# Input transposes of a TensorE-bound graph kernel: 128x128 on TensorE, or 32x32 blocks on VectorE behind a second, blocked load

## Chip, cores, metric

One core of one Trainium2 chip. The metric is the device time of one execution in microseconds, as the median of several; all runs told of here were in the fast state (granted TensorE clock 0.994 to 0.997 of full speed).

## The reference

Two graph layers on 64 graphs of 256 nodes with 256 features, all in float32. Layer 0 is a graph attention twice over (scores masked by `adj`, softmax over axis 1), a layer norm and a feed-forward part; layer 1 is attention with 8 heads, whose values depend on the relation `adj == r`, and a feed-forward part again. Cut to what uses the inputs:

```python
def _gat(h, adj, W, a, out_features):
    Wh = jnp.matmul(h, W)
    e = leaky_relu(Wh @ a[:F] + swapaxes(Wh @ a[F:], 1, 2), 0.2)
    att = softmax(where(adj > 0, e, NEG), axis=1)
    return jnp.matmul(att, Wh)
# layer 1
for r in range(4):
    mask = (adj_matrix == r)[:, None]
    out = out + einsum('bhij,bhjd->bhid', attn * mask, v_r)
```

## The kernel before

It takes two graphs at a time (a group, 512 nodes) and runs 32 turns. A turn works on three groups: on layer 1 of group y, layer 0 of group x, and the input and first attention of group z. The projection needs x with features on partitions (`xT`); both layers need the adjacency with the other node on partitions (`aT`). TensorE made both, sixteen 128x128 transposes for a group, into PSUM (where the results of TensorE land), and ScalarE or VectorE copied the result to SBUF (the memory in which the kernel keeps its tiles):

```python
def to_features(src, name, scale=None, shift=None):
    dst = work.tile([P, KB, TN], F32, tag="hT", name=name)
    for k in range(KB):
        ps = bank(f"{name}p{k}")
        for t in range(T):
            nc.tensor.transpose(ps[:, t * P:(t + 1) * P], src[:, t, k * P:(k + 1) * P], ident)
        ...  # VectorE: copy (or scale and shift) ps to dst
def adjacency(u, af):
    for b in range(G):
        ps = bank(f"aTp{u}_{b}")
        ...  # four TensorE transposes of af into ps
        nc.scalar.copy(aT[:, b * NB:(b + 1) * NB, :]..., ps)
    # check that every entry is 0 or 1 (the narrow path relies on it)
    nc.vector.scalar_tensor_tensor(a, a, 1.0, a, op0=ALU.subtract, op1=ALU.mult, accum_out=other[:, u:u + 1])
def early(z):
    d["aT"] = adjacency(z, d["af"])
    d["xT"] = to_features(d["xs"], f"xT{z}")
# the turn, from the middle on (order of TensorE):
#   hid 6,7 (h1p) -> early(z) -> apply 2, 3 (po, zo) -> out 0 (yop) -> project(z) (xpp) -> out 1 (yop) -> ...
```

`apply` ends in `divided` on VectorE: the reciprocal `rz` of `zo`, then `oT = po * rz`, which the second `yop` matmuls read.

Of the kernel before, what the change touches and what calls it, by code (L numbers as in the profile page):

```python
# [9 lines left out]
F32 = mybir.dt.float32  # L10
I32 = mybir.dt.int32
# [5 lines left out]
P = 128  # L17
# [368 lines left out]
def narrow_path(  # L386
# [13 lines left out]
    nc = tc.nc  # L400
    B, N, F = x.shape
# [3 lines left out]
    KB = F // P  # L405
    FB = FF // P
    NB = N // P
    G = 2
    T = G * NB
    TN = G * N  # L410
# [7 lines left out]
    io = ctx.enter_context(tc.tile_pool(name="io", bufs=2))  # L418
    work = ctx.enter_context(tc.tile_pool(name="work", bufs=2))
# [3 lines left out]
    def bank(name):  # L423
        return psum.tile([P, 512], F32, tag="g", name=name, bufs=6)


    def load(u):
        xs = io.tile([P, T, F], F32, tag="xs", name=f"xs{u}")
        nc.sync.dma_start(xs, x[G * u:G * (u + 1)].rearrange("b (c p) f -> p (b c) f", p=P))
        if u == 1:  # L430

            af = work.tile([P, FB, TN], F32, tag="h1", name=f"af{u}", bufs=1)
            af = af[:, 0:2, :].rearrange("p c (t n) -> p (c t) n", t=2)
        else:
            af = io.tile([P, T, N], F32, tag="af", name=f"af{u}", bufs=1)
        nc.gpsimd.dma_start(af, adj[G * u:G * (u + 1)].rearrange("b (c p) f -> p (b c) f", p=P))
        return xs, af


    ident = const.tile([P, P], F32, name="ident")  # L440
# [75 lines left out]

    gwe = gat_weights()
    g = {u: {} for u in range(NG)}
    for u in range(2):
        g[u]["xs"], g[u]["af"] = load(u)  # L520
    wf1, wf2 = weight(g_wf1, "wf1"), weight(g_wf2, "wf2")
    lg1, lb1, bf1, lg2, lb2, bq, bk, lg3, lb3, b1 = columns(
        (g_g1, g_b1, g_bf1, g_g2, g_b2, t_bq, t_bk, t_g1, t_be1, t_b1), "cols", nc.scalar)
# [20 lines left out]
# [7 lines that stand above are left out]
            if scale is None:  # L551
                nc.vector.tensor_copy(dst[:, k, :], ps)
            else:
                nc.vector.tensor_scalar(dst[:, k, :], ps, scale[:, k:k + 1], shift[:, k:k + 1],  # L554
                                        op0=ALU.mult, op1=ALU.add)
        return dst

    def adjacency(u, af):

        aT = work.tile([P, T, N], F32, tag="aT", name=f"aT{u}")  # L560
        for b in range(G):
            ps = bank(f"aTp{u}_{b}")
            for j in range(NB):
                for i in range(NB):
                    nc.tensor.transpose(ps[:, j * N + i * P:j * N + (i + 1) * P],  # L565
                                        af[:, b * NB + i, j * P:(j + 1) * P], ident)
            nc.scalar.copy(aT[:, b * NB:(b + 1) * NB, :].rearrange("p t n -> p (t n)"), ps)
        a = af.rearrange("p t n -> p (t n)")
        nc.vector.scalar_tensor_tensor(a, a, 1.0, a, op0=ALU.subtract, op1=ALU.mult,
                                       accum_out=other[:, u:u + 1])  # L570
        return aT

    def projected(u, hT):
        xp = work.tile([P, T, WX], F32, tag="wh", name=f"xp{u}")
# [179 lines left out]
    def early(z):  # L754

        d = g[z]
        d["aT"] = adjacency(z, d["af"])
        d["xT"] = to_features(d["xs"], f"xT{z}")

    def project(z):  # L760
        d = g[z]
# [6 lines left out]
    def second_scores(z):  # L768
        d = g[z]
        d["s"] = gat_softmax(z, 1, d["hp"], F, F, d["aT"])  # L770
# [38 lines left out]
    def turn(y_, x_, z):  # L809
        def have(u):  # L810
            return 0 <= u < NG

        if y_ == 0:
            g[z]["xs"], g[z]["af"] = load(z)
        if z + 1 < NG:
            g[z + 1]["xs"], g[z + 1]["af"] = load(z + 1)
        Y, X, Z = g.get(y_, {}), g.get(x_, {}), g.get(z, {})
        if have(y_):
            hT = to_features(Y["y"], f"h2T{y_}", lg2, lb2)
        if have(x_) and y_ > 0:  # L820
            second_sums(x_)
        if have(y_):
            q, k_ = queries_keys(y_, hT)
            v = values(y_, hT, range(T // 2))
        if have(x_):
            h1hT = to_features(X["y"], f"h1T{x_}", lg1, lb1)
        if have(y_):
            values(y_, hT, range(T // 2, T), v)
            quads = [(b, m) for b in range(G) for m in range(KB)]
            aT = Y["aT"]  # L830
            oT = work.tile([P, KB, TN], F32, tag="oT", name=f"oT{y_}", bufs=1)
            acc = [None] * G
            e = {}

            def scores(n):
                e[n] = weighted(y_, *quads[n], q, k_, aT)

            def apply_(n):
                b, m = quads[n]
                if m == 0:  # L840
                    acc[b] = [psum.tile([P, 512], F32, tag=t_, name=f"{t_}{y_}_{b}") for t_ in ("po", "zo")]
                applied(b, m, v, *e.pop(n), *acc[b])
                if m == KB - 1:
                    divided(y_, b, *acc[b], oT)

        h1 = None

        def steps():
            if have(y_):
                yield scores, 0  # L850
            yield hid, range(0, 3)
            if have(y_):
                yield scores, 1
                yield piece, None
                yield apply_, 0
            yield hid, range(3, 4)
            if have(y_):
                yield scores, 2
                yield apply_, 1
            yield hid, range(4, 6)  # L860
            if have(y_):
                yield scores, 3
                yield piece, None
            yield hid, range(6, 8)
            if have(z):
                yield early, z
            if have(y_):
                yield apply_, 2
                yield apply_, 3

        def hid(blocks):
            nonlocal h1
            if have(x_):
                h1 = hidden(x_, 0, h1hT, wf1, bf1, AF.Relu, blocks, h1)

        for do, what in steps():
            do(what)
        if have(y_):
            yo = work.tile([P, T, F], F32, tag="y", name=f"yo{y_}")

            def out_(b):
                add_blocks(y_, "yop", yo, Y["res"], b, lambda t, k: oT[:, k, t * P:(t + 1) * P],
                           lambda b, k: wo[:, k, :], KB)
            out_(0)
            piece()
        if have(z):
            project(z)
        if have(y_):
            out_(1)
        if have(z):  # L890
            first_scores(z)
        if have(y_):
            yn = normed(y_, 2, yo)
            res = affine(y_, 2, yn, rg3, rb3)
            piece()
        if have(x_):
            yf = hidden_out(x_, 0, h1, wf2, X["res"])
            X["y"] = normed(x_, 1, yf)
            X["res"] = affine(x_, 1, X["y"], rg2, rb2)
        if have(y_):  # L900
            hT = to_features(yn, f"h3T{y_}", lg3, lb3)
        if have(z):
            Z["hp"] = gat_first(z, Z["s"], Z["xp"])
        if have(y_):
            h1 = hidden(y_, 1, hT, w1, b1, AF.Gelu, range(FB))
        if have(z):
            second_scores(z)
        if y_ == NG - 2:
            left.append(out_pieces(y_, h1, res))
        elif y_ == NG - 1:  # L910
            for _ in out_pieces(y_, h1, res):
                pass
        else:
            yf = hidden_out(y_, 1, h1, w2, res)
            yn = normed(y_, 3, yf)
            res = affine(y_, 3, yn, rg4, rb4)
            nc.sync.dma_start(out[G * y_:G * (y_ + 1)].rearrange("b (c p) f -> p (b c) f", p=P), res)
# [2 lines left out]
        g[z]["hp"] = gat_first(z, g[z]["s"], g[z]["xp"])  # L920

    with tc.manual_schedule(engines={mybir.EngineType.PE}):
        for stage in (early, project, first_scores):
            stage(0)
        for stage in (early, project, first_scores):
            stage(1)
        for stage in (first_sums, second_scores):
            stage(0)
        for stage in (first_sums, second_scores):
            stage(1)  # L930
        second_sums(0)
        hT = to_features(g[0]["y"], "h1T0", lg1, lb1)
        h1 = hidden(0, 0, hT, wf1, bf1, AF.Relu, range(FB))
        yf = hidden_out(0, 0, h1, wf2, g[0]["res"])
        g[0]["y"] = normed(0, 1, yf)
        g[0]["res"] = affine(0, 1, g[0]["y"], rg2, rb2)
        second_sums(1)
        for u in range(NG):
            turn(u, u + 1, u + 2)
# [11 lines left out]
    ps = bank("goodp")  # L951
# [42 lines left out]
```

## Time and profile before

| | before |
|---|---|
| time, median of 6 (range) | 3344.96 us (3344.36 to 3345.93) |
| TensorE busy (share of the span) | 3298.2 us (99%) |
| VectorE / ScalarE / GpSimd busy | 54% / 32% / 30% |
| DMA queue q1, share of 16 engines | 3.8% |

A busy share tells which engine leaves least room; the chain that ended last tells whether the end of the program hangs on that engine. The prediction shows the lines. Mean durations of matmuls overlap, so what one costs in a stream is read from the starts of its neighbours, not from its duration. In a timeline, a bracket at the end of a line gives how long the engine was idle before it, and what ended that.

### The profile page before, as it was taken

How to read it: one execution, taken by the hardware profiler on the slowest of the kernel's cores; microseconds unless marked ns; L12 is line 12 of the kernel's file. 1: busy time of each engine (PE TensorE's matmuls, PEld its weight loads, DVE VectorE, ACT ScalarE, POOL GpSimd, SP SyncE). 2: the span in 40 equal slices, each digit the busy share in tenths (PEclk: the TensorE clock that was granted, in tenths of full speed). 3: DMA queues.
4: the chain of work that ended last, by engine and by line, in shares of the span. 5: the costliest groups of instructions: out<-in, count | busy, mean ns of one | idle time of the engine just before them, and what ended most of it. 6: DMA issues, size and time to landing. Idle time of an engine off the chain costs nothing.

```text
span 3342.7 us, 43294 instructions
## 1 busy us (share of the span) xinstructions
PE 3298.2 (99%) x17948; PEld 2160.2 (65%) x17948; DVE 1818.6 (54%) x3611; ACT 1083.8 (32%) x1920; POOL 987.4 (30%) x852
## 2 busy tenths in 40 slices
PE   7999999999999999999999999999999999999998
PEld 5666666666666666666666666666666666666655
DVE  3654556555556545565555565455654555654545
ACT  3233233332332333333323333333333233333321
POOL 2223323233232233232332322332323323223222
PEclk9999999999999999999999999999999999999999
DMA  4000000000000000000000000000000000000000
GB/s 131 14 19 14 20 7 20 20 13 20 7 20 20 20 13 20 7 20 20 13 20 7 20 20 20 13 18 8 20 20 13 20 7 20 20 14 12 1 7 14
DMA packets 57258, 60.92 MB, mean 18 GB/s; under 512 B 1976, under 2 KB 56416, under 8 KB 57056
## 3 DMA queue, kind: packets, MB, share of 16 engines
q1 hardware_dynamic: 39808, 41.03, 3.8%
q0 software_dynamic: 16896, 16.78, 2.3%
q8 instruction: 143, 2.34, 0.3%
q14 instruction: 59, 0.48, 0.0%
q10 hardware_dynamic: 352, 0.28, 0.0%
HBM read 41.31 MB, written 16.78 MB: 17 GB/s over the span
## 4 chain that ended last, share of the span: by engine, by line
PE 97%; DVE 1%; issue 1%; DMA 1%; POOL 0%; SPq 0%; ACT 0%; ACTq 0%; POOLq 0%; DVEq 0%
PE h1p L668 27%; PE yfp L627 25%; PE po L737 7%; PE vp L700 7%; PE sp L716 4%; PE yop L627 3%; PE qp L687 3%; PE hpp L616 3%; PE xpp L578 3%; PE kp L687 3%; PE ygp L627 3%; PE zo L740 2%; PE rows L588 1%; PE aTp L565 1%; PE yfp L794 1%
## 5 line engine op out<-in xcount | busy, mean ns | idle before, releaser
L670 ACT ACTIVATE h<-h1p,cols 128x512 f32<-128x512 f32 x512 | 353.2, 690 | 531.7 <-PE h1p L668 530.5
L668 PE MATMUL h1p<-h1T,wf 128*128 128x512 f32 x1024 | 474.5, 607 | 0.1
L627 PE MATMUL yfp<-wf,h 128*128 128x256 f32 x2048 | 447.3, 379 | 0.0
L668 PE MATMUL h1p<-h3T,w 128*128 128x512 f32 x1024 | 445.4, 592 | 1.8 <-DVE h3T L554 1.8
L724 DVE TENSOR_TENSOR ea<-e,aT 128x1024 f32<-128x1024 f32 x256 | 320.2, 1291 | 197.6 <-ACT e L722 197.6
L627 PEld LDWEIGHTS yfp<-wf,h 128*128 128x128 f32 x2048 | 386.8, 190 | 51.8 <-issue 0.5
L627 PE MATMUL yfp<-w,h 128*128 128x256 f32 x1920 | 419.4, 379 | 0.0
L627 PEld LDWEIGHTS yfp<-w,h 128*128 128x128 f32 x1920 | 362.5, 190 | 48.1
L722 ACT ACTIVATE e<-sp 128x512 f32<-128x512 f32 x512 | 264.3, 603 | 301.3 <-PE sp L716 300.0
L668 PEld LDWEIGHTS h1p<-h3T,w 128*128 128x128 f32 x1024 | 194.2, 190 | 234.2 <-issue 228.6
L746 POOL TENSOR_TENSOR low<-low,rz 128x512 f32<-128x512 f32 x64 | 82.2, 1284 | 891.0 <-DVE rz L745 891.0
L668 PEld LDWEIGHTS h1p<-h1T,wf 128*128 128x128 f32 x1024 | 184.9, 190 | 232.7 <-issue 190.6
L597 DVE SCALAR_TENSOR_TENSOR s<-s 128x512 f32<-128x512 f32 x128 | 87.1, 680 | 427.9 <-ACT s L594 426.6
L658 POOL TENSOR_TENSOR res<-res,rb 128x1024 f32<-128x1024 f32 (+1 forms) x130 | 301.3, 2317 | 10.2
L630 DVE TENSOR_TENSOR yf<-yfp,res 128x512 f32<-128x512 f32 x124 | 85.8, 692 | 394.8 <-PE yfp L627 393.6
L645 POOL TENSOR_TENSOR rs<-ve,mhalf 128x4 f32<-128x4 f32 (+1 forms) x130 | 131.6, 1012 | 411.9 <-DVE ve L644 411.8
L745 DVE RECIPROCAL rz<-zo 128x512 f32<-128x512 f32 x64 | 214.7, 3354 | 59.7 <-PE zo L740 59.6
L700 PE MATMUL vp<-wv,h2T 128*128 128x512 f32 x512 | 230.1, 592 | 0.0
L689 ACT ACTIVATE q<-qp,cols 128x512 f32<-128x512 f32 x64 | 44.0, 687 | 530.4 <-PE qp L687 530.4
L618 ACT COPY hp<-hpp 128x258 f32<-128x258 f32 x128 | 47.4, 376 | 423.6 <-PE hpp L616 423.6
L657 POOL TENSOR_TENSOR res<-yf,rg 128x1024 f32<-128x1024 f32 (+1 forms) x66 | 151.2, 2291 | 96.2 <-DVE yf L649 95.4
L700 PEld LDWEIGHTS vp<-wv,h2T 128*128 128x128 f32 x512 | 94.9, 190 | 107.6 <-issue 107.6
(494 smaller groups left out, 4351.1 us busy)
## 6 DMA issues: line engine op xcount, KB each, us to landing
xs<-in_x_dram SPq DMA_DIRECT2D x32, 512.0 KB, 3.9
af<-in_adj_dram POOLq DMA_DIRECT2D x32, 512.0 KB, 4.5
out_dram<-res SPq DMA_DIRECT2D x30, 512.0 KB
wf<-in_L_gnn_w_ff_dram SPq DMA_DIRECT2D x2, 1024.0 KB, 7.1
w<-in_L_gnn_W_dram SPq DMA_DIRECT2D x2, 1024.0 KB
out_dram<-res SPq DMA_DIRECT2D x4, 256.0 KB, 2.1
wv<-in_L_gnn_Wv_dram SPq DMA_DIRECT2D x2, 256.0 KB
gw<-in_L_gnn_W_dram ACTq DMA_DIRECT2D x1, 256.0 KB
```

Of the source, the lines that this page charges most:

```text
L627: nc.tensor.matmul(ps[:, i * F:(i + 1) * F], lhs(t, k), rhs(b, k), start=(k == 0), stop=(k == n - 1))
L657: nc.gpsimd.tensor_mul(r, xn, g[:, None, :].to_broadcast(list(r.shape)))
L658: nc.gpsimd.tensor_add(r, r, b[:, None, :].to_broadcast(list(r.shape)))
L668: nc.tensor.matmul(ps, wi[:, k, f * P:(f + 1) * P], hT[:, k, :], start=(k == 0), stop=(k == KB - 1))
L670: nc.scalar.activation(h1[:, f, :], ps, func, bias=bi[:, f:f + 1])
L687: nc.tensor.matmul(ps, w[:, k, m * P:(m + 1) * P], hT[:, k, :], start=(k == 0), stop=(k == KB - 1))
L700: nc.tensor.matmul(ps, hT[:, k, t * P:(t + 1) * P], wvf[:, k, :], start=(k == 0), stop=(k == KB - 1))
L716: nc.tensor.matmul(ps[a][:, j * N:(j + 1) * N], k_[hp, m, j0:j0 + P], q[hp, m, b * N:(b + 1) * N], start=True, stop=True)
L722: nc.scalar.activation(e[:, a, :], ps[a], AF.Exp, scale=isd)
L724: nc.vector.tensor_tensor(ea[:, a:a + 2, :], e[:, a:a + 2, :], ab[:, None, :].to_broadcast([P, 2, NB * N]), ALU.mult)
L737: nc.tensor.matmul(po[hp, m * N:(m + 1) * N], vs[:, hp], w[:, a, j * N:(j + 1) * N], start=(n == 0), stop=(n == len(terms) - 1))
L745: nc.vector.reciprocal(rz, zo)
```

## The change

Its intent is to take the input transposes of the middle turns off TensorE. The VectorE transpose that the kernel uses turns 32x32 blocks and leaves each within its 32 partitions. So the load does the moving between groups of partitions: for each quarter q of the partitions it brings pieces of 32 columns, so that the blocks that quarter needs lie beside one another; VectorE then transposes all blocks of a tile in one instruction. x is loaded a second time for this, since the residual needs it untransposed. The first two groups keep the old way.

```diff
 def load(u):
     xs = io.tile([P, T, F], F32, tag="xs", name=f"xs{u}")
     nc.sync.dma_start(xs, x[G * u:G * (u + 1)].rearrange("b (c p) f -> p (b c) f", p=P))
-    af = io.tile([P, T, N], F32, tag="af", name=f"af{u}", bufs=1)      # u == 1: in the h1 tile
-    nc.gpsimd.dma_start(af, adj[G * u:G * (u + 1)].rearrange("b (c p) f -> p (b c) f", p=P))
+    xq = io.tile([P, KB, TN], F32, tag="xq", name=f"xq{u}", bufs=1)
+    aq = io.tile([P, T, N], I32, tag="aq", name=f"aq{u}", bufs=1)
+    xu = x[G * u:G * (u + 1)].rearrange("b (n r) (k q c) -> q k r (b n) c", r=32, k=KB, c=32)
+    au = adj[G * u:G * (u + 1)].rearrange("b (n r) (j q c) -> q b r j n c", r=32, j=NB, c=32)
+    for q in range(Q):
+        qp = slice(q * 32, (q + 1) * 32)
+        for k in range(KB):
+            nc.sync.dma_start(xq[qp, k, :].rearrange("r (n c) -> r n c", c=32), xu[q, k])
+        for b in range(G):
+            nc.sync.dma_start(aq[qp, b * NB:(b + 1) * NB, :].rearrange("r j (n c) -> r j n c", c=32), au[q, b])
 def adjacency(u, aq):
+    aT = work.tile([P, T, N], I32, tag="aT", name=f"aT{u}")
+    nc.vector.transpose(aT..., aq...)
+    return aT
 def early(z):
-    d["aT"] = adjacency(z, d["af"])
-    d["xT"] = to_features(d["xs"], f"xT{z}")
+    d["xT"] = work.tile([P, KB, TN], F32, tag="hT", name=f"xT{z}")
+    nc.vector.transpose(d["xT"]..., d["xq"]...)
+    d["aT"] = adjacency(z, d["aq"])
# cut: load_first, early_first (groups 0 and 1 as before, both adjacency tiles in the h1 tile);
#      checked(), the check of the adjacency, now a function of its own;
-            oT = work.tile([P, KB, TN], F32, tag="oT", name=f"oT{y_}", bufs=1)
+            oT = q                                   # room for the new tiles
```

More of the change, by code (lines that the diff above doesn't have):

```diff
@@ L424, in bank @@
         return psum.tile([P, 512], F32, tag="g", name=name, bufs=6)
+    Q = P // 32
     def load(u):
@@ L429, in load, with load_first @@
         nc.sync.dma_start(xs, x[G * u:G * (u + 1)].rearrange("b (c p) f -> p (b c) f", p=P))
-        if u == 1:
-            af = work.tile([P, FB, TN], F32, tag="h1", name=f"af{u}", bufs=1)
-            af = af[:, 0:2, :].rearrange("p c (t n) -> p (c t) n", t=2)
-        else:
-            af = io.tile([P, T, N], F32, tag="af", name=f"af{u}", bufs=1)
-        nc.gpsimd.dma_start(af, adj[G * u:G * (u + 1)].rearrange("b (c p) f -> p (b c) f", p=P))
-        return xs, af
+        xq = io.tile([P, KB, TN], F32, tag="xq", name=f"xq{u}", bufs=1)
[7 more added lines that the diff above has]
+            for b in range(G):
+                nc.sync.dma_start(aq[qp, b * NB:(b + 1) * NB, :].rearrange("r j (n c) -> r j n c", c=32),
+                                  au[q, b])
+        return xs, xq, aq
+    def load_first():
+        h1 = work.tile([P, FB, TN], F32, tag="h1", name="first", bufs=1)
+        for u in range(2):
+            xs = io.tile([P, T, F], F32, tag="xs", name=f"xs{u}")
+            nc.sync.dma_start(xs, x[G * u:G * (u + 1)].rearrange("b (c p) f -> p (b c) f", p=P))
+            af = h1[:, 2 * u:2 * u + 2, :].rearrange("p c (t n) -> p (c t) n", t=2)
+            nc.gpsimd.dma_start(af, adj[G * u:G * (u + 1)].rearrange("b (c p) f -> p (b c) f", p=P))
+            g[u].update(xs=xs, aq=af)
     ident = const.tile([P, P], F32, name="ident")
@@ L518, in narrow_path @@
     g = {u: {} for u in range(NG)}
-    for u in range(2):
-        g[u]["xs"], g[u]["af"] = load(u)
+    load_first()
     wf1, wf2 = weight(g_wf1, "wf1"), weight(g_wf2, "wf2")
@@ L556, in to_features, with adjacency, early_first @@
         return dst
-    def adjacency(u, af):
-        aT = work.tile([P, T, N], F32, tag="aT", name=f"aT{u}")
+    def adjacency(u, aq):
+        aT = work.tile([P, T, N], I32, tag="aT", name=f"aT{u}")
+        nc.vector.transpose(aT.rearrange("p t n -> p (t n)"), aq.rearrange("p t n -> p (t n)"))
+        return aT
+    def early_first(z):
+        d = g[z]
+        d["aT"] = work.tile([P, T, N], I32, tag="aT", name=f"aT{z}")
         for b in range(G):
-            ps = bank(f"aTp{u}_{b}")
+            ps = bank(f"aTp{z}_{b}")
             for j in range(NB):
@@ L565, in adjacency, with checked @@
                     nc.tensor.transpose(ps[:, j * N + i * P:j * N + (i + 1) * P],
-                                        af[:, b * NB + i, j * P:(j + 1) * P], ident)
-            nc.scalar.copy(aT[:, b * NB:(b + 1) * NB, :].rearrange("p t n -> p (t n)"), ps)
-        a = af.rearrange("p t n -> p (t n)")
+                                        d["aq"][:, b * NB + i, j * P:(j + 1) * P], ident)
+            nc.scalar.copy(d["aT"][:, b * NB:(b + 1) * NB, :].rearrange("p t n -> p (t n)"), ps)
+        d["xT"] = to_features(d["xs"], f"xT{z}")
+    def checked(u, aq):
+        a = aq.rearrange("p t n -> p (t n)")
         nc.vector.scalar_tensor_tensor(a, a, 1.0, a, op0=ALU.subtract, op1=ALU.mult,
                                        accum_out=other[:, u:u + 1])
-        return aT
     def projected(u, hT):
@@ L756, in early @@
         d = g[z]
-        d["aT"] = adjacency(z, d["af"])
-        d["xT"] = to_features(d["xs"], f"xT{z}")
+        d["xT"] = work.tile([P, KB, TN], F32, tag="hT", name=f"xT{z}")
+        nc.vector.transpose(d["xT"].rearrange("p k n -> p (k n)"), d["xq"].rearrange("p k n -> p (k n)"))
+        d["aT"] = adjacency(z, d["aq"])
     def project(z):
@@ L813, in turn @@
         if y_ == 0:
-            g[z]["xs"], g[z]["af"] = load(z)
+            g[z]["xs"], g[z]["xq"], g[z]["aq"] = load(z)
         if z + 1 < NG:
-            g[z + 1]["xs"], g[z + 1]["af"] = load(z + 1)
+            g[z + 1]["xs"], g[z + 1]["xq"], g[z + 1]["aq"] = load(z + 1)
         Y, X, Z = g.get(y_, {}), g.get(x_, {}), g.get(z, {})
@@ L907, in turn @@
             second_scores(z)
+            checked(z, Z["aq"])
         if y_ == NG - 2:
@@ L922, in narrow_path @@
     with tc.manual_schedule(engines={mybir.EngineType.PE}):
-        for stage in (early, project, first_scores):
+        for stage in (early_first, project, first_scores):
             stage(0)
-        for stage in (early, project, first_scores):
+        for stage in (early_first, project, first_scores):
             stage(1)
@@ L930, in narrow_path @@
             stage(1)
+        for u in range(2):
+            checked(u, g[u]["aq"])
         second_sums(0)
```

## The prediction

> **What bounds the kernel now.** I read the page's busy shares first, then the chain that ended last, then TensorE's groups and the timeline of one middle turn on TensorE and on VectorE, and last the groups of the work that the change touches.
>
> Busy shares, the slices and the chain, from the page of the kernel before:
>
> ```profile
> span 3342.7 us, 43294 instructions
> PE 3298.2 (99%) x17948; PEld 2160.2 (65%) x17948; DVE 1818.6 (54%) x3611; ACT 1083.8 (32%) x1920; POOL 987.4 (30%) x852
> ...
> PEclk9999999999999999999999999999999999999999
> DMA  4000000000000000000000000000000000000000
> ...
> PE 97%; DVE 1%; issue 1%; DMA 1%; POOL 0%; SPq 0%; ACT 0%; ACTq 0%; POOLq 0%; DVEq 0%
> ```
>
> TensorE is busy for 3298 of 3343 us and makes up 97% of the chain, at full granted clock. VectorE is at 54% and the DMA engines are near idle after the start. So the time is the sum of what TensorE issues, and an instruction taken off it is worth its own time as long as nothing else becomes late. That 44 us of idle TensorE is nearly all in the first 60 us and the last two turns, where this change does nothing.
>
> What the removed instructions cost comes from the timeline of TensorE in one middle turn (columns: start us, us, what), at the place where the input transposes stand:
>
> ```profile
> 1565.70 3.70 PE L668 MATMUL h1p<-h1T,wf 128*128 128x512 f32 x8
> 1569.24 1.04 PE L565 MATMUL aTp<-ident,af 128*128 128x128 f32 x8
> 1570.11 1.04 PE L550 MATMUL xT16p<-ident,xs 128*128 128x128 f32 x8
> 1571.08 1.07 PE L737 MATMUL po<-e,v 128*32 128x256 f32 x16
> ```
>
> A single transpose is listed at about 272 ns, but they are pipelined: eight of them move the next start by 0.87 us, 109 ns each. From the first transpose to the first `po` is 1571.08 - 1569.24 = 1.84 us. Other turns that I looked at (starting at 239, 648, 1160, 2592 and 3104 us) show the same 1.84. A turn lasts 102.3 us (the `xT` copies start that far apart), so this is 1.8% of a turn.
>
> The last turn but one has no new inputs to transpose, so it already shows the order that the changed kernel will have:
>
> ```profile
> 3202.64 3.70 PE L668 MATMUL h1p<-h1T,wf 128*128 128x512 f32 x8
> 3206.28 1.07 PE L737 MATMUL po<-e,v 128*32 128x256 f32 x16
> ```
>
> From `h1p` to `po` it takes 3.64 us there, against 5.38 us in the middle turn: 1.74 us less, and TensorE does not wait for ScalarE or VectorE at that place.
>
> **What the Trainium skill says.** "TensorE: Matmul & The Clock Gate", Part 4, gives about 275 ns for a TensorE transpose in one kernel's context and says that PSUM is the destination, so that a copy must follow. The trace agrees on the duration (median 273 ns) and shows the copies; but the cost in a stream is the 109 ns above, and the trace decides. "VectorE: DVE Perf Modes", The three transpose paths, says that VectorE transposes only within 32x32 blocks; that is why the load has to place the blocks. "Vector Engine (DVE) Microarchitecture Reference", 3.8, says that this is pipelined to one element per cycle per lane; no transpose of VectorE is in the trace before. "DMA: Bandwidth & Descriptors", in its opening table, wants 512 B and more for full rate; the new pieces are 32 columns of 4 B, 128 B. The trace before has nearly only larger packets, so it cannot confirm this.
>
> **The change part by part.** There are 32 groups; groups 0 and 1 still go through TensorE, so 30 are changed.
>
> TensorE loses 8 + 8 transposes in each of 30 turns, and gains nothing. By the pair of timelines that is 30 x 1.74 = 52 us (by the bare transposes 30 x 1.84 = 55 us). Everything else in its order stays.
>
> ScalarE loses two PSUM copies of `aT` for each group (591 ns each); it is not on the chain, so this is worth nothing by itself.
>
> VectorE loses two PSUM copies of `xT` (0.68 us each, 1.36 us for a group) and gets two block transposes of 128x1024. I take for one what a plain 1024-element operation costs:
>
> ```profile
> L727 DVE TENSOR_TENSOR es<-e 128x1024 f32<-128x1024 f32 x128 | 155.8, 1217 | 0.0
> L569 DVE SCALAR_TENSOR_TENSOR af<-af 128x1024 f32<-128x1024 f32 x32 | 38.8, 1213 | 1.5 <-PE aTp L565 1.5
> ```
>
> So 2 x 1.2 = 2.4 us come and 1.36 go: about 1 us more for a turn of 100, still far from full. The check of the adjacency stays at 1.2 us. What matters is its place. In the built order of the changed kernel the `xT` transpose stands before the first `ea`, where VectorE waited 1.48 us for ScalarE anyway in the turn shown. The `aT` transpose and the check stand between the last `es` and the last reciprocal `rz`:
>
> ```profile
> 1570.20 1.21 DVE L727 TENSOR_TENSOR es<-e 128x1024 f32<-128x1024 f32 x1
> 1571.34 1.21 DVE L569 SCALAR_TENSOR_TENSOR af<-af 128x1024 f32<-128x1024 f32 x1
> 1572.48 0.08 DVE L569 DVE_READ_ACCUMULATOR af<-af 128x1 f32 x1
> 1572.48 1.28 DVE L552 COPY xT<-xT16p 128x512 f32<-128x512 f32 x2
> 1575.67 3.36 DVE L745 RECIPROCAL rz<-zo 128x512 f32<-128x512 f32 x1 [1.91 <-PE zo L740]
> 1578.94 0.63 DVE L630 TENSOR_TENSOR yo<-yop,res 128x512 f32<-128x512 f32 x1
> 1579.49 0.68 DVE L747 TENSOR_TENSOR oT<-po,rz 128x512 f32<-128x512 f32 x1
> ```
>
> Before, the check and the two copies filled 2.4 us and then VectorE idled 1.91 us for `zo`. After, the transpose and the check fill about 2.4 us too, from 1571.4 to 1573.8, and `zo` comes 1.74 us earlier, at about 1573.9. They meet: the idle time of VectorE is used up and nothing is late. From the start of `rz` to the end of `oT` it takes 4.5 us (1575.67 to 1580.17), and TensorE has `yop` and `xpp` to do meanwhile, 5.3 us (1575.53 to 1580.87). So there is some 0.7 us of slack before the second `yop` waits.
>
> DMA: `x` is loaded a second time, and both in pieces of 128 B: 2 x 4096 pieces for a group. Before, queue q1 took 3.8% of 16 engines' span for 39808 packets, 0.038 x 16 x 3342.7 us / 39808 = 51 ns for one of mostly 1 KB. My estimate for a 128 B piece is between the same 51 ns and twice that: 8192 x 51 / 16 = 26 us, up to 52 us, for a turn. In the built order `xq` is free for its next load when its transpose is done, and `aq` after its check, both of which are needed again one turn, about 100 us, later. So the transfers are hidden. GpSimd no longer issues the adjacency loads of the middle turns; it is off the chain as well.
>
> Sum: 3345.0 - 52.2 = 3292.8; I say 3292, a ratio of 0.984.
>
> **The rivals.** (1) VectorE comes late. If a block transpose of 4-byte elements takes 2.4 us and not 1.2, `rz` starts some 1.2 us late, the 0.7 us of slack is gone, and TensorE waits about 0.5 us in each of 30 turns: 15 us back, about 3307. For it speaks that the slack is small and that no such instruction has been timed here; against it the skill's one element per cycle. A slower `ea` or score product because `aT` is now an integer tile would act in the same way; I see no reason for it.
>
> (2) The loads come late. VectorE works in order, so a transpose that waits for its DMA stops everything behind it. It needs more than 100 us for 16 transfers, 200 ns for a piece, four times what the 1 KB packets took. Then each turn would be as long as its transfers: 130 us of them would make 4100 us. Against it stands the factor of four, and that the queue is otherwise hardly used. A milder form is that instruction fetches, which use the same engines, are delayed.
>
> (3) More is won than TensorE's own time: less work on ScalarE, no load descriptors on GpSimd, fewer PSUM buffers passing. But middle turns have next to no idle TensorE to win back, so this is bounded to a few us, some 3285.
>
> **Range and chances.** TensorE's share is read twice (52 and 55 us) and is sure to within some 5 us; the rivals add mostly on the slow side. The threshold of 2% is 66.9 us, more than TensorE loses in work, so faster by over 2% needs 12 us from elsewhere: 0.06. Slower by over 2% needs rival (2): 0.04. Within 2%: 0.90. The range that should hold it 8 times in 10 is 3284 to 3309.
>
> **What would show it.** Right: TensorE's busy time falls to about 3245 us and its share stays at 98% or more; a middle turn lasts 100.5 us; `po` follows `h1p` directly after 3.6 us; the block transposes take 1.2 us each; the DMA share in middle slices rises from 0 to between 2 and 5 tenths; ScalarE's two `aT` copies are gone. Rival (1) would show as idle time before `yop` or `po` with VectorE's `oT` or `ea` as releaser, 0.3 us or more in each turn. Rival (2) would show as a wait of VectorE for the DMA of `xq` or `aq`, and a DMA share of 9 tenths. I would be wrong outright if TensorE's other groups got slower (means other than 379, 592 or 607 ns), for instance because many small writes disturb its reads.

## The result, and the profile after

| | before | after |
|---|---|---|
| time, median of 6 (range) | 3344.96 us (3344.36 to 3345.93) | 3293.15 us (3291.81 to 3294.51) |
| ratio, 95% interval | | 0.9844, 0.9832 to 0.9857 |
| TensorE busy | 3298.2 us | 3244.5 us |
| VectorE busy | 1818.6 us | 1853.9 us |
| q1, share of 16 engines | 3.8% | 10.0% |

A ratio here is the mean time of one kernel's runs over that of the other's in the same rounds, so not quite the ratio of the medians quoted. The difference of 52 us is real, since the ranges are far apart.

The page of the kernel after, busy shares, DMA slices (tenths of the 16 engines) and chain:

```profile
span 3290.2 us, 42867 instructions
PE 3244.5 (99%) x17468; PEld 2105.4 (64%) x17468; DVE 1853.9 (56%) x3611; ACT 1050.6 (32%) x1860; POOL 960.7 (29%) x822
...
DMA  5110001101011100011010111000110101110000
...
PE 96%; DVE 1%; issue 1%; DMA 1%; POOL 0%; SPq 0%; ACT 0%; ACTq 0%; POOLq 0%; DVEq 0%
```

There are 480 matmul records fewer, 16 for each of 30 groups. TensorE is as full as before, at 99%, so its work alone still sets the time; the span fell by 52.5 us and TensorE's busy time by 53.7.

TensorE's timeline in one middle turn of the kernel after (start us, us, what), at the place of the transposes and on to the second `yop`:

```profile
1540.18 3.70 PE L695 MATMUL h1p<-h1T,wf 128*128 128x512 f32 x8
1543.81 1.07 PE L764 MATMUL po<-e,v 128*32 128x256 f32 x16
...
1547.72 0.61 PE L767 MATMUL zo<-es,ones 128*32 128x256 f32 x8
1548.27 1.99 PE L654 MATMUL yop<-wo,q 128*128 128x256 f32 x8
1550.10 3.67 PE L605 MATMUL xpp<-gwe,xT 128*128 128x260 f32 x16
1553.60 1.89 PE L654 MATMUL yop<-wo,q 128*128 128x256 f32 x8
```

From `h1p` to `po` it is now 3.63 us, as in the old kernel's last turn but one. No line carries a bracket, so TensorE waits for nothing. VectorE's timeline of the same turn:

```profile
1544.69 1.21 DVE L754 TENSOR_TENSOR es<-e 128x1024 f32<-128x1024 f32 x1
1545.83 1.23 DVE L579 STREAM_TRANSPOSE aT<-aq 128x1024 int32<-128x1024 int32 x1
1547.09 1.23 DVE L597 SCALAR_TENSOR_TENSOR aq<-aq 128x1024 int32<-128x1024 int32 x1
1548.25 0.08 DVE L597 DVE_READ_ACCUMULATOR aq<-aq 128x1 f32 x1
1548.40 3.36 DVE L772 RECIPROCAL rz<-zo 128x512 f32<-128x512 f32 x1
1551.68 0.63 DVE L657 TENSOR_TENSOR yo<-yop,res 128x512 f32<-128x512 f32 x1
1552.22 0.68 DVE L774 TENSOR_TENSOR q<-po,rz 128x512 f32<-128x512 f32 x1
```

The block transpose takes 1.23 us. The 1.91 us that VectorE idled ahead of `rz` are gone, and the product (`oT`, now in the tile `q`) ends at 1552.90, 0.70 us before TensorE begins the second `yop`. This is the new tightest place. The other transpose, ahead of the first `ea` of a turn:

```profile
1621.79 1.25 DVE L785 STREAM_TRANSPOSE xT<-xq 128x1024 f32<-128x1024 f32 x1
1623.23 2.36 DVE L751 TENSOR_TENSOR ea<-e,aT 128x1024 f32<-128x1024 f32 x2 [0.20 <-ACT e L749]
```

It fills idle time: 0.20 us of it are left here, against 1.48 in the turn shown of the kernel before:

```profile
1650.50 2.36 DVE L724 TENSOR_TENSOR ea<-e,aT 128x1024 f32<-128x1024 f32 x2 [1.48 <-ACT e L722]
```

`ea` reads the adjacency as an integer tile now and takes 1291 ns on average in both kernels; the score product with `aT` takes 421 ns against 422. So the slowing of these two that the prediction named did not come. Nor did TensorE's other groups get slower: the three that it named have means of 379, 593 and 606 ns.

### The profile page after: what moved, and what is told of

It is laid out like the page before. It is cut to its first block, busy times and chain, and to the rows that moved or that the text cites. A ratio compares the mean times of both kernels' runs of the same rounds, so it can differ in the third digit from the quotient of the medians.

```text
span 3290.2 us, 42867 instructions
## 1 busy us (share of the span) xinstructions
PE 3244.5 (99%) x17468; PEld 2105.4 (64%) x17468; DVE 1853.9 (56%) x3611; ACT 1050.6 (32%) x1860; POOL 960.7 (29%) x822
## 4 chain that ended last, share of the span: by engine, by line
PE 96%; DVE 1%; issue 1%; DMA 1%; POOL 0%; SPq 0%; ACT 0%; ACTq 0%; POOLq 0%; DVEq 0%
PE h1p L695 27%; PE yfp L654 26%; PE po L764 7%; PE vp L727 7%; PE sp L743 4%; PE yop L654 3%; PE qp L714 3%; PE hpp L643 3%; PE xpp L605 3%; PE kp L714 3%; PE ygp L654 3%; PE zo L767 2%; PE rows L615 1%; PE yfp L822 1%; DVE rz L772 0%
## 5 line engine op out<-in xcount | busy, mean ns | idle before, releaser
L751 DVE TENSOR_TENSOR ea<-e,aT 128x1024 f32<-128x1024 f32 x256 | 320.2, 1291 | 162.9 <-ACT e L749 162.9
```

The lines of the kernel that those rows point to most:

```text
L751: nc.vector.tensor_tensor(ea[:, a:a + 2, :], e[:, a:a + 2, :], ab[:, None, :].to_broadcast([P, 2, NB * N]), ALU.mult)
```

## The experiments

The theory: TensorE's time is the sum of what it issues, the transposes' own 1.74 us in each turn are the whole gain, and what replaces them lies beside it. Three rivals were tried: that relief of other engines is part of the gain, that VectorE has room (or has none) by its amount of work, and that short DMA pieces cost something. All kernels gave correct results except `piece512`.

### The transposes put back on TensorE alone

```diff
 def early(z):
     ...
     d["aT"] = adjacency(z, d["aq"])
+    for k in range(2 * KB):
+        ps = bank(f"idle{z}_{k}")
+        for t in range(T):
+            nc.tensor.transpose(ps[:, t * P:(t + 1) * P], d["xs"][:, t, k % KB * P:(k % KB + 1) * P], ident)
```

> The changed kernel with 16 TensorE transposes put back into each of 30 middle turns at the old place, into PSUM buffers that nobody reads: no copies come back on ScalarE or VectorE, and the block transposes stay. Theory (TensorE's own time is the whole gain): 3293 + 30 x 1.74 = 3345 us, the time of the kernel before. Rival (relief of ScalarE, GpSimd or of the PSUM copies is part of the gain): clearly under 3345, by the part that they gave.

3344.79 us, ratio to the kernel before 0.9999 (0.9983 to 1.0016). The whole 52 us came back, although ScalarE, GpSimd and VectorE kept the work of the changed kernel. Its TensorE timeline:

```profile
1567.29 3.70 PE L695 MATMUL h1p<-h1T,wf 128*128 128x512 f32 x8
1570.82 1.91 PE L790 MATMUL idle<-ident,xs 128*128 128x128 f32 x16
1572.66 1.07 PE L764 MATMUL po<-e,v 128*32 128x256 f32 x16
```

The same 5.37 us from `h1p` to `po` as in the kernel before (5.38). So relief of other engines is no part of the gain that could be told: the median is 1 us under that of the kernel before in this call, and the interval leaves room for some 5.

### Half of the change at a time

`adj_only`, in which only the adjacency goes through VectorE and x is transposed by TensorE again:

```diff
-    d["xT"] = work.tile(...); nc.vector.transpose(d["xT"]..., d["xq"]...)
     d["aT"] = adjacency(z, d["aq"])
+    d["xT"] = to_features(d["xs"], f"xT{z}")       # and no xq tile, no loads of it
```

> Only the adjacency goes through VectorE's block transpose; x is transposed by TensorE again, with its two VectorE copies, and is not loaded twice. Theory: half of the gain, 3345 - 26 = 3319 us; VectorE has 3.7 us of work before rz but TensorE is 0.87 us later, so there is no new wait. Rival (late VectorE): up to 10 us more.

3319.75 us, ratio 0.9924 (0.9907 to 0.9940): 25.4 us under the 3345.18 of the kernel before.

`x_only`, the other half: the load casts the adjacency to float32 as before, and TensorE transposes it.

```diff
+    aq = io.tile([P, T, N], F32, ...); nc.gpsimd.dma_start(aq, adj[...]...)    # in place of the small loads
 def adjacency(u, aq):
-    nc.vector.transpose(aT..., aq...)
+    ...  # TensorE transposes into ps, nc.scalar.copy to aT, as before
```

> Only x goes through VectorE's block transpose; the adjacency is cast by its load, transposed by TensorE and copied by ScalarE as before. Theory: half of the gain, 3319 us. Rival (ScalarE's two copies hold TensorE up): adj_only gains more than x_only by some us.

3320.60 us, ratio 0.9925 (0.9908 to 0.9941): 24.6 us. The halves are alike and add up to 50 of the 52 us; a rest of 2 us is within the spread of these runs. ScalarE's copies, which only `x_only` keeps, make no difference that could be told.

### How much more VectorE could do, and where

```diff
 def adjacency(u, aq):
-    nc.vector.transpose(aT..., aq...)
+    for _ in range(2):                              # late1; range(3) in late2
+        nc.vector.transpose(aT..., aq...)
```

> The block transpose of the adjacency done twice in each middle turn, between es and the last reciprocal rz: 1.26 us more on VectorE there. Theory (slack of 0.55 to 0.70 us before the second yop): TensorE waits 0.56 to 0.71 us in each of 30 turns, 3310 to 3314 us, with oT as releaser of yop. Rival (VectorE, at 56%, has room for it): 3293 us.

3311.49 us, ratio to the kernel before 0.9899 (0.9883 to 0.9916): 18 us over the changed kernel, 0.61 us for each of 30 turns. The second `yop` of a turn in `late1`:

```profile
1564.03 1.97 PE L655 MATMUL yop<-wo,q 128*128 128x256 f32 x8 [0.40 <-DVE q L775]
```

It starts 4.07 us after `xpp` (at 1559.96), against 3.50 in the kernel after (1550.10 to 1553.60): 0.57 us later. The chain that ended last changes with it: TensorE has 78% of it and VectorE 17%, against 96% and 1%, though TensorE is still busy for 98% of the span.

> The same transpose three times: 2.52 us more at that place. Theory: the wait grows by the full 1.26 us per turn over late1, 38 us: 3347 to 3352 us. Rival (VectorE has room): 3293 us.

3351.69 us, ratio 1.0021 (1.0004 to 1.0038): 40 us more than `late1`, 1.34 us a turn, about the length of one transpose. TensorE's timeline in `late2` shows the wait:

```profile
1577.68 3.67 PE L606 MATMUL xpp<-gwe,xT 128*128 128x260 f32 x16
1583.02 1.97 PE L655 MATMUL yop<-wo,q 128*128 128x256 f32 x8 [1.67 <-DVE q L775]
```

The bracket names VectorE's product as the releaser. Its 1.67 us count from the end that the profile models for `xpp`; by the starts, `yop` comes 5.34 us after `xpp` against 3.50, so 1.84 us late, while the whole program lost 1.95 us a turn against the changed kernel. The same amount of work at the other place:

```diff
 def early(z):
-    nc.vector.transpose(d["xT"]..., d["xq"]...)
+    for _ in range(3):
+        nc.vector.transpose(d["xT"]..., d["xq"]...)
```

> The block transpose of x three times in each middle turn, before the first ea: the same 2.5 us of VectorE work as in late2, at another place. Theory (place counts, not amount: the first ea and es would then be done at about 1628 and 1629 us of the turn shown, where TensorE reads them at 1629.3 and 1630.2): 3293 us, at most 5 more. Rival (amount of VectorE work counts): like late2, near 3350 us.

3293.67 us, ratio 0.9848 (0.9832 to 0.9865): nothing lost. The two kernels' busy lines, `late2` first:

```profile
PE 3254.4 (97%) x17468; PEld 2104.4 (63%) x17468; DVE 1926.5 (58%) x3671; ACT 1050.7 (31%) x1860; POOL 960.8 (29%) x822
```

and `early2`:

```profile
PE 3245.5 (99%) x17468; PEld 2106.2 (64%) x17468; DVE 1925.7 (59%) x3671; ACT 1051.5 (32%) x1860; POOL 962.0 (29%) x822
```

VectorE is as busy in one as in the other, and 58 us lie between their times. So the change is hidden by its place, with some 0.65 us to spare between `rz` and the second `yop`, and not by VectorE's low share.

### The loads

```diff
-    for q in range(Q):
-        ...
+    for _ in range(4):
+        for q in range(Q):
+            ...
```

> Every small load of x and of the adjacency issued four times over: 64 in place of 16 in each turn, the same data. Theory (transfers are hidden, some 10 us of 100 in use): 3293 us unchanged, with the queue's share up from 10.0% to some 27%. Rival (short pieces already load the DMA engines so that instruction fetches or other transfers are late): slower, by 20 us or more.

3292.70 us, ratio 0.9841 (0.9825 to 0.9858): 64 loads a turn cost nothing either. Queue q1 took 28.3%.

```diff
-    xu = x[...].rearrange("b (n r) (k q c) -> q k r (b n) c", r=32, k=KB, c=32)
+    xu = x[...].rearrange("b (n m r) (k c) -> m k r (b n) c", r=32, m=4, k=KB)     # c = 128; au in the same way
```

> The same bytes loaded in pieces of 128 columns, 512 B, in place of 32 columns, 128 B: wrong results on purpose, since the block transposes then find the wrong blocks. Theory (piece size is hidden): 3293 us. The trace tells what a piece costs: 51 ns or more for 128 B, as the prediction took, against about 12 ns that the queue's 10.0% works out to.

3292.89 us, ratio 0.9841 (0.9825 to 0.9857). The queue's line (packets, MB, share of the 16 engines' time), for the kernel after:

```profile
q1 hardware_dynamic: 293248, 72.52, 10.0%
```

for `loads4`:

```profile
q1 hardware_dynamic: 1053568, 166.98, 28.3%
```

and for `piece512`:

```profile
q1 hardware_dynamic: 108928, 72.52, 7.3%
```

`loads4` has 3 x 245760 more pieces of 128 B than the kernel after and takes (0.283 x 3293.7 - 0.100 x 3290.2) x 16 us = 9650 us more of the DMA engines: 13 ns for a piece. (The packets differ by 23040 more than that, 16 for each of the 1440 added transfers; their time is counted in.) Taking 245760 x 13.1 ns from the 5264 us of the kernel after leaves 2045 us for everything else on that queue. In `piece512` (span 3292.4 us) the 61440 pieces of 512 B then have 3846 - 2045 = 1800 us, 29 ns each. In bytes for time the short piece is the worse one, 9.8 against 17.5 GB/s for each engine, but it is cheap.

### TensorE's idle time at the start

The trace after shows one long wait at the start that has nothing to do with the change: TensorE stands for 8.1 us before `xpp` of group 1, because VectorE, working in order, waits 9.3 us for the weights `wv`. (In the kernel before the same two waits are 7.65 and 8.84 us.) `wv_pool` moves the two subtractions behind that wait to GpSimd.

```diff
-    nc.vector.tensor_tensor(wv[:, :, 1, :], wv[:, :, 1, :], wv[:, :, 0, :], ALU.subtract)
-    nc.vector.tensor_tensor(rbv[:, F:], rbv[:, F:], rbv[:, :F], ALU.subtract)
+    nc.gpsimd.tensor_tensor(wv[:, :, 1, :], wv[:, :, 1, :], wv[:, :, 0, :], ALU.subtract)
+    nc.gpsimd.tensor_tensor(rbv[:, F:], rbv[:, F:], rbv[:, :F], ALU.subtract)
```

The changed kernel ran beside it again:

> The changed kernel itself, once more, beside the next one on the same chip: 3293 us.

3293.17 us (3291.58 to 3294.30), ratio to the kernel before 0.9847.

> The changed kernel with the two subtractions on the loaded value weights moved from VectorE to GpSimd. In the changed kernel's trace VectorE, which works in order, waits 9.3 us for the load of wv in the start, and TensorE idles 8.1 us behind it, before the xpp of group 1. Theory (TensorE's idle time at the start is on the path as its work is): up to 7 us less, 3286 to 3290 us. Rival (that idle time only moves to the next wait of the start, which is bound by the loads or by GpSimd, where the subtractions now stand ahead of the scaling of xp): 3293 us or more.

3287.74 us (3286.09 to 3288.26), ratio 0.9832 (0.9818 to 0.9845). The ranges of the two do not overlap, so the 5.4 us between them are real, though the intervals of the ratios overlap. The timeline of the kernel after:

```profile
32.00 5.26 PE L605 MATMUL xpp<-gwe,xT 128*128 128x260 f32 x16 [8.08 <-DVE xT L570]
```

and of `wv_pool`:

```profile
26.91 5.62 PE L605 MATMUL xpp<-gwe,xT 128*128 128x260 f32 x16 [3.22 <-DVE xT L570]
```

The wait shrank by 4.9 us and the time by about as much. The time thus follows TensorE's idle time as it follows its work. This is the fastest version found.

## Why the prediction was right

3292 was predicted, 3293.15 measured. By its steps:

- **TensorE is the bound.** Shown: `te_back` changes TensorE's work alone and moves the time by 51.6 us, the whole gain; `loads4`, `piece512` and `early2` change other work and leave it within 0.6 us.
- **1.74 us a turn, not the duration of a transpose.** Shown: the changed kernel's block transposes of x start 100.56 us apart on average ((3029.5 - 113.2) / 29), against 102.3 us for the copies before. Sixteen times the listed 272 ns would have been 4.4 us a turn, 131 us in all. The right figure came from a turn of the old kernel that has no transposes.
- **VectorE: 1.2 us for a block transpose, 0.7 us of slack.** Shown: 1.23 and 1.25 us, and 0.70 us between the product's end and `yop` in the trace. `late1` puts the usable slack a little lower: 1.26 us more cost 0.61, so some 0.65 us were free. The first rival, a transpose of 2.4 us, is what `late1` imitates; it made 3311, and the prediction had said 3307 for it. VectorE's busy time rose by 35 us, where about 1 us a turn, 30 in all, had been worked out.
- **The loads are hidden.** The conclusion held, but its term was mis-sized. A 128 B piece was taken at 51 to 102 ns, which made 26 to 52 us a turn and 2 to 5 tenths in the DMA slices; the runs show 13 ns, 8192 x 13 / 16 = 7 us a turn, and slices of 0 and 1. The time per packet of long packets was carried over to short ones as if it did not depend on the length.
- **Nothing to win beyond TensorE's own time.** Shown for the middle turns by `te_back`. The 44 us of idle TensorE at the start and the end were called untouched by this change, which is so, but they can be won in part, as `wv_pool` shows.

## What to carry to other kernels

When one engine is busy 99% of the time, price what leaves it by the shift of its neighbours' starts, best from a stretch of the same kernel that lacks the work, and price what comes to other engines by where it stands in their order: 2.5 us of VectorE work a turn were free at one place and cost 58 us at another. A layout problem that a compute engine cannot solve alone (blocks in the wrong partitions) can be handed to the loads if these are needed only a turn later. A low busy share of an engine is no slack; the distance from its result to the instruction that reads it is.

## What the Trainium skill lacked or had wrong

- "VectorE: DVE Perf Modes", The three transpose paths: has 311 ns for a 128x128 bfloat16 transpose, and no time for 4-byte types. Measured here: 1.24 us for 128x1024 in float32 and 1.23 us in int32, as long as a plain float32 operation of that size on SBUF (1.22 us). This fits the one element per cycle and lane of "Vector Engine (DVE) Microarchitecture Reference", 3.8, but no trace here shows VectorE's cycle.
- "TensorE: Matmul & The Clock Gate", Part 4: its 275 ns in a kernel's context, beside a figure for bfloat16, is the duration, and 272 ns is what the trace lists here for float32; but in a stream of float32 transposes the starts are 109 ns apart, which the part does not say and which is what counts in a full engine.
- "DMA: Bandwidth & Descriptors", opening table: wants 512 B for full rate and says that below it there is read-modify-write. Here a 128 B piece of a load from HBM to SBUF took 13 ns of its DMA engine and a 512 B piece 29 ns: slower for its bytes by 1.8. The table gives no cost of a piece by its size; a count of cycles for a packet by its size stands further down the page, under "Why small descriptors are slow (HBM only)", and the prediction did not use it. No run here tests that count.
